# Moving one depthwise convolution's matmuls to the next slot, and the 5x5 convolution's transfers to one fixed point of each step

## The chip, the cores and the metric

The kernel runs on one core of a Trainium2 chip. The metric is the device time of one execution in microseconds (us); lower is better. PE is TensorE (matmuls, with PEld for its weight loads), DVE is VectorE, ACT is ScalarE, POOL is GpSimd and SP is SyncE. PE, DVE and ACT compute; SP and POOL issue nearly all the transfers here. [...]

## What is computed

The input is eight images of 32 channels by 128 x 128 pixels in float32. Two layers follow each other, each adding to its input. Cut to what matters:

```python
# layer 0
g    = group_norm(x)
xb   = patch_match_stack(g)        # per pixel, the 8 best of 25 shifts, gathered: 256 channels
dct  = conv1x1(xb, dct_w, groups=32)
h    = relu(depthwise3x3(conv1x1(xb, w1), w2))
h    = relu(depthwise3x3(conv1x1(h, w3), w4))
wien = sigmoid(depthwise3x3(conv1x1(h, w5), w6))
x    = x + conv1x1(conv1x1(wien * dct, inv_dct_w, groups=32), agg_w)
# layer 1
x    = x + conv5x5_each_channel(group_norm(x), kernel)
```

The three pairs (1x1, then depthwise 3x3) are called convolutions 1, 2 and 3 below. The product with `dct` and the aggregation that follows are the final part; layer 1 is the 5x5 convolution.

## The kernel before, in words

The work is a software pipeline over steps. A step `s` takes 8 rows of an image; an image has 17 steps (`NS + 1`), and there are 136 steps and two more to drain. In each step the loop `for i in (3, 2, 1, 0)` (L1026) runs four slots, named by `i`. Slot 3 runs the 1x1 of convolution 3 for the rows of two steps earlier, slot 2 that of convolution 2 for one step earlier, slot 1 that of convolution 1, and slot 0 the final part of two steps earlier. Every slot also gathers pixels for a later step.

The 256 channels of each convolution are halved. One half is depthwise-filtered on DVE: `pointwise_v` (L631, matmuls `pv`) puts it through ACT copies (L649) into a padded tile `tv`, `depthwise_v` (L681) runs nine taps, one on ACT (L692) and eight on DVE (L695), and L699 applies the activation. The other half is filtered on PE: `pointwise_t` (L651, matmuls `p`) goes through ACT copies (L672) into `t`, two SP transfers (L677, L679) copy rows of `t` to other partitions, and `depthwise_t` (L703) then runs 24 matmuls (L718, `pw<-t,dwd`), here called the taps of that convolution on PE. ACT evacuates them (L731), and SP copies two rows on (L620). After the DVE taps SP also copies two rows of `tv` (L627).

The taps on PE run one slot after their 1x1: generator `dt` is advanced twice per slot, once for the matmuls and once for L731 and L620. So convolution 3's taps stand in slot 2, convolution 2's in slot 1, convolution 1's in slot 0, and slot 3 has none. In PE's queue the slots are, without the tasks described next:

- slot 3: `pv` of convolution 3, `pa` (aggregation of the final part, L798), `p` of convolution 3, gather `pg` (L603)
- slot 2: `pv` and `p` of convolution 2, `pg`, taps of convolution 3
- slot 1: `pv` and `p` of convolution 1, `pg`, taps of convolution 2
- slot 0: `pc` (the grouped DCT, L777), `pg`, taps of convolution 1

All of `pv`, `p`, `pg`, `pc` and `pa` take turns in five PSUM buffers (`ps_x`, L71); the taps have two of their own (`ps_dw`, L193). DVE multiplies `pc` into the result (L785) in slot 0, and adds `pa` (L806) in slot 3.

Everything else, the search of the next image and the 5x5 of the image before, is cut into generator tasks. A task yields the letter of a queue and a cost, and is queued there: D for DVE, A for ACT, P and Q for PE. `run` (L222) takes tasks out. In each slot P runs after `pv`, then Q, then `tick` (L984) runs D tasks up to a credit (a share of 0.4 in slot 0, 0.2 in the others), then A. So a DVE task of slot 0 (a difference of images L413, costs L477 to L489, places L520 to L529, the 5x5's normalisation L864) is followed by its ACT part (such as the squares, L421) in slot 0, and by its PE part (`pd` L428, `pt` L494, `pi` L538, the 5x5's `p` L891) in slot 3.

The 5x5 (`layer1`, L815) takes eight channels at a time, four times per image: loads on POOL (`xy`, `xm`, L852 to L857), normalisation, matmuls, an add on DVE (L903) and four stores on POOL (L905), 62 rows each. The loads of the next eight channels reuse the two `xy` buffers that the stores read. For the last image (`last`) the loads are made at once.

PE, DVE and ACT keep the order in which the program was written (`ORDERED`, L14). POOL and SP do not: the tile scheduler orders their instructions by when it believes them ready.

Of the kernel before, what the change touches and what calls it, by code (L numbers as in the profile page):

```python
# [15 lines left out]
P = 128  # L16
# [26 lines left out]
def bm3d_conv_preact(  # L43
# [16 lines left out]
    nc = tc.nc  # L60
# [86 lines left out]
    with tc.tile_pool(name="setup", bufs=1) as sp, tc.tile_pool(  # L147
# [23 lines left out]
        for name, w in (("w1", w1), ("w3", w3), ("w5", w5)):  # L171
            t = sp.tile([P, 2, CK], F32, name=f"nat_{name}", tag=f"nat_{name}")
            nc.sync.dma_start(t, w.rearrange("(m p) i a b -> p m (i a b)", p=P))
            if name == "w1":

                nat, t = t, sp.tile([P, 2, CK], F32, name="w1_kc")
# [29 lines left out]

    queues = {"D": deque(), "A": deque(), "P": deque(), "Q": deque()}

    PAIR = 1.95
    pairs = [0]
# [9 lines left out]
    def run(which, credit=1e9):  # L222

        q, took = queues[which], 0.0
        for _ in range(len(q) if which != "D" else 1000):

            i = next(
                (
                    i
                    for i, (c, _, at) in enumerate(q)  # L230
                    if at <= now[0] and (c != PAIR or pairs[0] < 2)
                ),
                None,
            )
            if i is None or took >= credit:
                break
            cost, task, _ = q[i]
            del q[i]
            took += cost
            pairs[0] += cost == PAIR  # L240
            push(task)
        if which == "Q":
            pairs[0] = 0
        return took
# [570 lines left out]
    def layer1(b):  # L815

        yield "D", 0.2
        mv = work.tile([P, 2], F32, name=f"mv1_{b}", tag="mv1")
        nc.vector.bn_aggr(mv, stats[b].rearrange("p a b -> p (a b)"))
        mr = yield from group_stats(mv, f"b{b}")  # L820
        dg = work.tile([C, 2, C], F32, name=f"dg_{b}", tag="dg")
        for i in range(2):
            nc.vector.tensor_scalar(
                dg[:, i], ident[:C, :C], mr[:C, i : i + 1], None, op0=ALU.mult
            )
        yield "P", 0
        pb = ps_x.tile([P, 512], F32, name=f"pb_{b}", tag="x")
        nc.tensor.matmul(
            pb[:, : 2 * C], ones, dg.rearrange("p a b -> p (a b)"), start=True, stop=True
        )  # L830
        bc = work.tile([P, 2, C], F32, name=f"bc_{b}", tag="bc")
        nc.scalar.copy(bc.rearrange("p a b -> p (a b)"), pb[:, : 2 * C])
        last = b == NB - 1
        if last:
            ends = xnp.tile([P, HR, HX], F32, name="ends", tag="xn")
            ends = ends.rearrange("p r x -> p (r x)")[:, : 8 * 4 * W]
            ends = ends.rearrange("p (g c x) -> p g c x", g=8, x=W)
        xys = {}

        def load(c):  # L840


            if last:
                m = work.tile([P, 2, 4, W], F32, name=f"xo_{c}", tag="sel", bufs=4)
                t = [ends[:, c // 4], ends[:, c // 4 + 1], m[:, 0], m[:, 1]]
            else:
                t = [
                    work.tile([P, 4, W], F32, name=f"{name}_{b}_{c}_{e}", tag=name)
                    for name, e in (("xy", 0), ("xm", 0), ("xy", 1), ("xm", 1))
                ]  # L850
            src = x1d[b].rearrange("c y x -> y c x")
            nc.gpsimd.dma_start(t[0], src[:, c : c + 4])  # L852
            for h in range(2):
                nc.gpsimd.dma_start(
                    t[1][64 * h : 64 * h + 64], src[64 - 64 * h : P - 64 * h, c + 4 : c + 8]
                )
            nc.gpsimd.dma_start(t[2], src[:, c + 4 : c + 8])  # L857
            xys[c] = t

        def normalise(c):  # L860
            t = xys[c]
            for e in range(2):
                for i in range(4):
                    nc.vector.tensor_scalar(  # L864
                        t[3 - 2 * e][:, i],
                        t[e][:, i],
                        bc[:, 0, c + 4 * e + i : c + 4 * e + i + 1],
                        bc[:, 1, c + 4 * e + i : c + 4 * e + i + 1],
                        op0=ALU.subtract,
                        op1=ALU.mult,  # L870
                    )

        for c in range(0, C if last else 8, 8):
            load(c)
        push(middle(b, mr))
        for c in range(0, C, 8):
            if c == 0 or not last:
                yield "D", 2.0, 1 if last else 3
                normalise(c)
            yield "P", 0  # L880
            ps = [
                ps_x.tile([P, 4, W], F32, name=f"p5_{b}_{c}_{e}", tag="x") for e in range(2)
            ]
            t = xys.pop(c)

            for k, dx in enumerate((0, -2, -1, 1, 2)):
                xa, xz = max(0, -dx), min(W, W - dx)
                for h in range(2):
                    for e in range(2):
                        r, o = 64 * h, 64 * ((h + e) % 2)  # L890
                        nc.tensor.matmul(  # L891
                            ps[e][o : o + 64, :, xa:xz],
                            band[r : r + 64, dx + 2, r : r + 64],
                            t[3 - 2 * e][r : r + 64, :, xa + dx : xz + dx],
                            start=k == 0,
                            stop=k == 4,
                        )
            yield "D", 3.6 if last else 1.6
            if last and c + 8 < C:
                normalise(c + 8)  # L900
            for e in range(2):
                y = t[2 * e]
                nc.vector.tensor_add(y, y, ps[e])  # L903
                for a, z in ((0, 62), (66, P)):
                    nc.gpsimd.dma_start(  # L905
                        out[b, c + 4 * e : c + 4 * e + 4, a:z].rearrange("c y x -> y c x"),
                        y[a:z],
                    )
            if c + 8 < C and not last:
                yield "A", 0, 1  # L910
                load(c + 8)

        done.add((b, 0))

    def middle(b, mr):

        df = work.tile([P, SR, HX], F32, name=f"mid_{b}", tag="mid", bufs=1)
        for r in range(4):
            nc.gpsimd.dma_start(
                df[C * r : C * (r + 1), 0:5, 2 : 2 + W], x1d[b][:, 60 + r : 65 + r]  # L920
            )
        nc.gpsimd.memset(df[:, :, 0:2], 0.0)
        nc.gpsimd.memset(df[:, :, 2 + W :], 0.0)
        acc = df[:, 5, 2 : 2 + W]
        yield "D", 2.6, 4
        nc.vector.tensor_copy(acc, df[:, 2, 2 : 2 + W])
        nc.vector.tensor_scalar(
            df[:, 0:5, 2 : 2 + W],
            df[:, 0:5, 2 : 2 + W],
            mr[:, 0:1],  # L930
            mr[:, 1:2],
            op0=ALU.subtract,
            op1=ALU.mult,
        )
        for dy in range(5):
            if dy in (2, 4):
                yield "D", 2.0
            for dx in range(5):
                nc.vector.scalar_tensor_tensor(
                    acc,  # L940
                    df[:, dy, dx : dx + W],
                    kb[:, 5 * dy + dx : 5 * dy + dx + 1],
                    acc,
                    op0=ALU.mult,
                    op1=ALU.add,
                )
        for r in range(4):
            nc.gpsimd.dma_start(out[b, :, 62 + r], acc[C * r : C * (r + 1)])
        done.add((b, 1))
# [34 lines left out]
    def tick(b, i):  # L984

        now[0] += 1
        owed[0] += total / (NS - 2 if b else NS - 6) * (0.4 if i == 0 else 0.2)
        owed[0] -= run("D", owed[0]) if owed[0] > 0 else 0
        owed[0] = min(owed[0], 6.0)

    def until(cond, credit):
        while not cond():
            now[0] += 1
            run("D", credit)
            run("A")
            run("P")
            run("Q")

    with tc.manual_schedule(engines=ORDERED):
# [10 lines left out]

        dt = dv = kept = iter(())

        later = iter(())

        for s in range(len(steps) + 2):
# [10 lines left out]
            for i in (3, 2, 1, 0):  # L1026
                si = s - (i - 1 if i else 2)
                live = 0 <= si < len(steps)
                new_v = new_t = iter(())
                if live:  # L1030
                    bi, ni = steps[si]

# [13 lines left out]
                    final_dct(bi, ni, accs[3, bi, ni], xf, j0, j1)  # L1046

                run("Q")
                if s < len(steps):
                    unit(gather_select, u + 1, (0,))  # L1050
                    unit(gather_load, u + 3)
                    tick(b, i)
                next(later, None)
                next(new_v, None)
                if live and i:
# [1 line left out]
                next(kept, None)  # L1057
                if s < len(steps):
                    unit(gather_pixels, u)
                next(dt, None)  # L1060
                run("A")
                next(dv, None)
                if s < len(steps):
# [74 lines left out]
```

## Time and profile before

| | |
|---|---|
| median of 3 runs | 6853.36 us (6853.05 to 6886.87) |
| profiled execution | 6856.73 us, its span 6855.0 us |
| mean granted TensorE clock | 0.974 |
| PE busy | 6362.1 us, 93% |
| DVE busy | 5857.0 us, 85% |
| ACT busy | 5067.7 us, 74% |
| POOL busy | 3250.0 us, 47% |
| transfers | 1019.84 MB, mean 149 GB/s |
| taps on PE, L718 | 2161.7 us busy, 137.9 us idle just before |
| taps on DVE, L695 | 4032.8 us busy |

The page gives the busy time of an engine, groups of instructions by line with their mean duration, and the idle time of the engine just before them with what ended it. A view of the waits says who waited for whom, and a view in order of time shows single slots. One image in the steady part takes some 825 us: two successive first steps of an image stand at 1943 and 2768 us.

### The profile page before, as it was taken

What the parts mean: (1) busy time and instruction counts of PE and PEld (TensorE: products, weight loads), DVE (VectorE), ACT (ScalarE), POOL (GpSimd) and SP (SyncE); (2) the same over time, 40 slices, a digit from 0 to 9 for tenths busy, and PEclk for the clock granted to TensorE, in tenths of its full rate; (3) what the DMA queues carried; (4) which work ended last, traced back from release to release, by engine and by line L of the source; (5) the groups of instructions that cost most, each with busy time, mean ns of one, the idle gap of its engine ahead of it and who ended that gap; (6) DMA issues with size and microseconds to landing.
All of it is one profiled execution on the core that took longest, in us unless ns stands there. A gap on an engine that the chain in (4) does not pass through costs nothing.

```text
span 6855.0 us, 232443 instructions
## 1 busy us (share of the span) xinstructions
PE 6362.1 (93%) x101090; PEld 2969.2 (43%) x101090; DVE 5857.0 (85%) x8822; ACT 5067.7 (74%) x6698; POOL 3250.0 (47%) x5351
## 2 busy tenths in 40 slices
PE   4698899999999999999999999999999999999997
PEld 1344444444444444444444444444444444444443
DVE  6799988989889898988989888898988889877776
ACT  4687768777687777877778777887768777786772
POOL 6345436544464444644446444464445544344334
PEclk9899999999999999999999999999999999999998
DMA  3566656666566675665656656566665666566553
GB/s 80 134 151 148 155 134 150 163 149 162 149 155 161 147 168 134 167 145 151 165 131 165 160 145 167 134 172 152 151 153 146 161 157 149 137 164 157 148 151 79
DMA packets 809531, 1019.84 MB, mean 149 GB/s; under 512 B 255456, under 2 KB 619936, under 8 KB 808512
## 3 DMA queue, kind: packets, MB, share of 16 engines
q0 software_dynamic: 422432, 745.61, 42.4%
q1 hardware_dynamic: 381056, 256.86, 16.9%
q8 instruction: 796, 13.04, 0.8%
q10 hardware_dynamic: 5024, 2.49, 0.2%
q14 instruction: 223, 1.83, 0.1%
HBM read 553.25 MB, written 217.01 MB: 112 GB/s over the span
## 4 chain that ended last, share of the span: by engine, by line
PE 53%; DVE 20%; DMA 9%; ACT 8%; issue 6%; POOL 3%; SPq 0%; ACTq 0%; POOLq 0%; DVEq 0%
PE pw L718 19%; PE pv L641 13%; DVE acc L695 13%; PE p L665 11%; DMA t<-t 4%; PE pg L603 3%; PE pc L777 2%; PE p L891 2%; DVE idx L506 2%; ACT ib L588 2%; DVE df L413 1%; PE pd L428 1%; ACT df L421 1%; PE pa L798 1%; DVE acc L785 1%
## 5 line engine op out<-in xcount | busy, mean ns | idle before, releaser
L695 DVE SCALAR_TENSOR_TENSOR acc<-tv,dwv,acc 128x1024 f32<-128x1024 f32 (+3 forms) x3264 | 4032.8, 1237 | 255.1 <-ACT acc L692 141.7
L718 PE MATMUL pw<-t,dwd 96*32 96x508 f32 (+6 forms) x19392 | 2161.7, 593 | 137.9 <-DMA t<-t 97.4
L574 POOL DMA_DIRECT2D ib<-idxd x1024 | 571.8, 559 | 1828.0 <-ACT sel L589 1677.2
L718 PEld LDWEIGHTS pw<-t,dwd 96*32 96x32 f32 (+1 forms) x19392 | 715.7, 112 | 1265.5 <-issue 1174.2
L588 ACT ACTIVATE ib<-ib,nplace 128x1024 bf16<-128x1024 bf16 x1024 | 1170.3, 1143 | 19.1 <-DMA ib<-idxd 19.1
L589 ACT ACTIVATE sel<-ib 128x1024 f32<-128x1024 bf16 x1024 | 1084.7, 1059 | 32.5
L665 PE MATMUL p<-acc,lw 128*32 128x256 f32 x16768 | 991.3, 381 | 20.0 <-ACT tv L649 19.5
L641 PE MATMUL pv<-acc,lw 128*128 128x512 f32 (+1 forms) x2112 | 972.0, 602 | 30.2 <-DVE acc L785 22.9
L758 POOL DMA_DIRECT2D xf<-xbd x1088 | 652.8, 634 | 305.3 <-PE pc L777 80.7
L665 PEld LDWEIGHTS p<-acc,lw 128*32 128x32 f32 x16768 | 556.6, 111 | 447.8 <-ACT tv L649 59.5
L649 ACT COPY tv<-pv 128x512 f32<-128x512 f32 (+2 forms) x784 | 439.2, 578 | 403.4 <-PE pv L641 380.6
L603 PEld LDWEIGHTS pg<-sel,xt 128*32 128x32 f32 x45056 | 575.3, 111 | 260.4 <-ACT sel L589 67.1
L421 ACT ACTIVATE df<-df 128x786 f32<-128x786 f32 (+2 forms) x576 | 468.5, 860 | 291.6 <-DVE df L413 288.5
L603 PE MATMUL pg<-sel,xt 128*32 128x48 f32 x45056 | 593.5, 207 | 89.2 <-ACT sel L589 47.6
L731 ACT ACTIVATE acc<-pw 128x512 f32<-128x512 f32 (+2 forms) x808 | 442.7, 573 | 295.7 <-PE pw L718 294.9
L641 PEld LDWEIGHTS pv<-acc,lw 128*128 128x128 f32 x2112 | 380.0, 191 | 524.3 <-issue 404.4
L413 DVE TENSOR_TENSOR df<-xn 128x786 f32<-128x786 f32 (+2 forms) x576 | 527.8, 968 | 82.8 <-PE pd L428 70.9
L699 ACT ACTIVATE acc<-acc 128x1024 f32<-128x1024 f32 (+3 forms) x408 | 416.9, 1022 | 235.4 <-DVE acc L695 235.1
L672 ACT COPY t<-p 128x512 f32<-128x512 f32 x800 | 424.7, 571 | 127.8 <-PE p L665 125.8
L692 ACT ACTIVATE acc<-tv,dwv 128x1024 f32<-128x1024 f32 (+3 forms) x408 | 454.6, 1114 | 57.9 <-PE pa L798 39.1
L641 PE MATMUL pv<-xb,lw 128*128 128x512 f32 x1024 | 474.5, 606 | 0.0
L665 PE MATMUL p<-xb,lw 128*32 128x256 f32 x8192 | 467.6, 380 | 0.0
(151 smaller groups left out, 5778.6 us busy)
## 6 DMA issues: line engine op xcount, KB each, us to landing
ib<-idxd POOLq DMA_DIRECT2D x1024, 256.0 KB, 4.5
xbd<-xb POOLq DMA_DIRECT2D x128, 1024.0 KB, 6.8
xf<-xbd POOLq DMA_DIRECT2D x960, 128.0 KB, 7.0
t<-t SPq DMA_DIRECT2D x792, 128.0 KB
t<-t SPq DMA_DIRECT2D x384, 256.0 KB
tv<-tv SPq DMA_DIRECT2D x384, 130.0 KB
xt<-xtd POOLq DMA_DIRECT2D x240, 176.0 KB, 4.4
xl<-xs POOLq DMA_DIRECT2D x256, 64.0 KB, 2.5
```

Of the source, the lines that this page charges most:

```text
L413: nc.vector.tensor_sub(df[:, :, ca:cz], xn[:, r0 : r0 + SR, ca:cz], xn[:, r0 + dy : r0 + dy + SR, ca + dx : cz + dx],)
L421: nc.scalar.activation(df[:, :, ca:cz], df[:, :, ca:cz], AF.Square)
L574: nc.gpsimd.dma_start(ib.rearrange("p k y x -> p (k y x)"), idxd[b][s4 // 8, s4 % 8, 4 * k0 : 4 * k0 + 8] .rearrange("k x -> (k x)") .part ...
L588: nc.scalar.activation(ib, ib, AF.Square, bias=nplace)
L589: nc.scalar.activation(sel, ib, AF.Relu, scale=-1.0, bias=1.0)
L603: nc.tensor.matmul(pg[C * j : C * (j + 1), :, xa:xz], xt[:, t], sels[j // 2][:, j % 2, :, xa:xz], start=True, stop=True,)
L641: nc.tensor.matmul(ps[:, :hr], lhsT[:, g, P:CK], src(g)[:, h : h + hr], start=g == 0, stop=g == 1,)
L665: nc.tensor.matmul(ps[C * r : C * (r + 1), e, :nb], lhsT[:, g, s], rows[:, r : r + 4 * nb - 3 : 4], start=g == 0, stop=g == 1,)
L692: nc.scalar.activation(acc, rows, AF.Copy, scale=tap)
L695: nc.vector.scalar_tensor_tensor(acc, rows, tap, acc, op0=ALU.mult, op1=ALU.add)
L718: nc.tensor.matmul(pt[u][C * j : C * (j + 1), : nh[u], :nb, xa:xz], dwd[0:hi, i - 1, u, j, dx + 1], t[0:hi, j, : nh[u], :nb, xa + dx : xz ...
L758: nc.gpsimd.dma_start(xf[p : p + C, m, j0:j1], src[g, m, (h + m + 1) % 2, :, :, ya:yz])
```

## The change

Two things are moved; no arithmetic is added or removed.

- The taps of convolution 1 leave slot 0. Their generator is kept as `first_t` and advanced in slot 3 of the next step: the matmuls after the P and Q tasks and before `p` of convolution 3, the evacuation (L731) and the row copy (L620) after `tick`.
- A fifth queue, S, takes the 5x5's stores and loads (not those of the last image, but with the stores of its `middle` rows). It is run when slot 2 begins, and in `until`. Loads of the next eight channels come one S later than the stores. The two adds of L903 now stand together ahead of the stores.

```diff
-    queues = {"D": deque(), "A": deque(), "P": deque(), "Q": deque()}
+    queues = {"S": deque(), "D": deque(), "A": deque(), "P": deque(), "Q": deque()}
...
+        if not last:
+            yield "S", 0
         for c in range(0, C if last else 8, 8):
             load(c)
...
             for e in range(2):
+                nc.vector.tensor_add(t[2 * e], t[2 * e], ps[e])
+            if not last:
+                yield "S", 0
+            for e in range(2):
                 y = t[2 * e]
-                nc.vector.tensor_add(y, y, ps[e])
                 for a, z in ((0, 62), (66, P)):
                     nc.gpsimd.dma_start(
...
             if c + 8 < C and not last:
-                yield "A", 0, 1
+                yield "S", 0, 1
                 load(c + 8)
...
+        yield "S", 0
         for r in range(4):
             nc.gpsimd.dma_start(out[b, :, 62 + r], acc[C * r : C * (r + 1)])
...
             run("D", credit)
+            run("S")
             run("A")
...
+        first_t = iter(())
...
                 new_v = new_t = iter(())
+                if i == 2:
+                    run("S")
...
                 run("Q")
+                if i == 3:
+                    next(first_t, None)
                 if s < len(steps):
                     unit(gather_select, u + 1, (0,))
                     unit(gather_load, u + 3)
                     tick(b, i)
+                if i == 3:
+                    next(first_t, None)
...
-                next(dt, None)
+                if i:
+                    next(dt, None)
+                else:
+                    first_t, dt = dt, iter(())
                 run("A")
```

## The prediction

> **What bounds the kernel now.** I read the page's busy times first, then the waits of PE and DVE, then one step in order of time. Page:
>
> ```profile
> PE 6362.1 (93%) x101090; PEld 2969.2 (43%) x101090; DVE 5857.0 (85%) x8822; ACT 5067.7 (74%) x6698; POOL 3250.0 (47%) x5351
> ```
>
> PE is the bound: some 493 us of the 6855.0 are all it doesn't work in, and a stall of PE is paid in full unless it replaces another. Who PE and DVE waited for (total us, times, longest):
>
> ```profile
> PE pw L718 <- DMA t<-t: 97.4, 39, 5.1
> PE pd L428 <- ACT df L421: 42.9, 38, 2.9
> PE pv L641 <- DVE acc L785: 22.9, 15, 2.2
> PE p L665 <- ACT tv L649: 19.5, 7, 3.7
> ```
>
> and of DVE's waits the largest:
>
> ```profile
> DVE xr L806 <- PE pa L798: 311.8, 68, 15.7
> ```
>
> The taps' largest wait is for the row copies of `t`. I sorted PE's timeline by slots. Of 136 tap groups in slot 0, 16 came over 0.6 us late: 54.5 us idle before them, and 34.9 us by which they ran longer than the usual 5.33 us. In slot 2 it is 73.2 and 38.8 us (33 groups), in slot 1 almost nothing. One such step (start, duration, the wait in brackets), from slot 1's taps to slot 3's tasks:
>
> ```profile
> 3080.03 5.33 PE L718 MATMUL pw<-t,dwd 96*32 96x512 f32 x48
> 3085.30 1.95 PE L777 MATMUL pc<-xf,ldct 64*64 64x512 f32 x16
> 3087.17 1.12 PE L603 MATMUL pg<-sel,xt 128*32 128x48 f32 x88
> 3091.98 7.96 PE L718 MATMUL pw<-t,dwd 96*32 96x512 f32 x48 [3.69 <-DMA t<-t]
> 3099.87 3.70 PE L641 MATMUL pv<-acc,lw 128*128 128x512 f32 x8
> 3103.50 1.07 PE L798 MATMUL pa<-acc,lagg 128*32 128x256 f32 x16
> 3104.51 0.44 PE L538 MATMUL pi<-cst,oc 128*128 128x128 f32 x2
> ```
>
> SP's copies for slot 0's taps:
>
> ```profile
> 3079.78 0.59 SPq L677 DMA_DIRECT2D t<-t  x1
> 3080.41 1.68 SPq L679 DMA_DIRECT2D t<-t  x1
> ```
>
> POOL, with the stores of the 5x5:
>
> ```profile
> 3074.99 6.08 POOL L905 DMA_DIRECT2D out_dram<-xy  x4 [2.64 <-DVE xy L903]
> 3088.86 0.78 POOL L852 DMA_DIRECT2D xy<-x1d  x1 [7.79 <-DMA out_dram<-xy]
> ```
>
> DVE's product of the final part and the places of the search, and ACT's squares:
>
> ```profile
> 3087.13 2.48 DVE L785 TENSOR_TENSOR acc<-acc,pc 128x512 f32<-128x512 f32 x4
> 3095.49 0.42 DVE L529 TENSOR_TENSOR oc<-oc,cst 128x256 f32<-128x256 f32 x1
> ```
> ```profile
> 3092.17 1.74 ACT L421 ACTIVATE df<-df 128x786 f32<-128x786 f32 x2 [3.22 <-DVE df L413]
> ```
>
> The reader is to see two things. The stores go out at 3075, the row copies five us later take until 3092, and slot 0's taps wait. And the 5.33 us of taps between `pg` and `pv` are also what lets DVE and ACT finish slot 0's work before slot 3 needs it.
>
> **What the Trainium skill says.** "DMA: Bandwidth & Descriptors", section Issuing engines are not separate DMA queues: transfers of SP and POOL run on the same 16 DMA engines and interleave. The trace agrees: the SP copies above are late while POOL's stores are open. Same page, Why a DMA increments its semaphore by 16 and not by 1: a transfer is spread over the largest number up to 16 that divides its slowest dimension; 62 rows give 2 engines. The trace fits: a store of 124 KB lands in 10.9 us (median), a load of 256 KB on 128 rows in 4.1. "TensorE: Matmul & The Clock Gate", Part 1: the HAM clock gate: after an idle window TensorE runs slower until it has been busy again. The trace: after gaps of 2.5 us and more PE lost 1.6 to 2.7 us more in what followed, after shorter ones 0.4 to 0.6.
>
> **Part 1, removed: slot 0's waits.** Convolution 1's taps come behind `pv` (3.7) and `pa` (1.07), 4.8 us later; the longest wait there was 5.1. So 54.5 + 34.9 less 4.9 that waited for ACT: **-85**.
>
> **Part 2, removed: the old idle time of slot 3**, which is re-made below or covered by the taps now ahead of `p`: 23.1 (L785), 19.5 (L649), 13.8 (L421), 9.8 (`pi`), 14.4 (`pg`, no releaser shown): **-81**.
>
> **Part 3, added: `pv` of slot 3 comes straight behind slot 0's `pg`.** It takes the PSUM buffer that DVE's first L785 frees. From slot 1's start to that release: `pv` and ACT 5.5, eight DVE taps 10.5, L785 0.7 = 16.7. PE needs 13.4 for a bare slot 1 and 3.0 for slot 0 = 16.4. So 0.3 us a step where no task fills these slots, and less where one does. In the trace many L785 are up to 7.5 us later; since slot 3 grows by 5.3 us, I let DVE catch up that much. Over 125 steps this leaves 25 (no lateness but the excess over 5.33) to 80; I take **+45**.
>
> **Part 4, added: slot 3's tasks lose their cover.** They wait for DVE and ACT work of slot 0, and the taps come behind them. In the step shown, PE would be free at 3088.29 + 3.7 + 1.07 = 3093.0, while the places (L529) end at 3095.9: 2.9 us. The same sum for each of the 125 steps, DVE lateness taken off as in part 3, gives 104 us (14 an image: 2.4, 2.6, 3.1, 2.1, 1.7, ... and zeros). The instruction order of the changed kernel has other tasks in slot 0, among them an add, the middle rows and a cost block in one tick (8.4 us of DVE) ahead of a transposition. My count for one image is 13 to 17. **+104** (70 to 125). Some 60 such gaps slow what follows by 0.4: **+25** (10 to 40).
>
> **Part 5, SP's queue.** The order of the changed kernel has, in 108 of 128 steps, the `tv` copy of convolution 3 (L627) ahead of its `t` copies (L677, L679); in 12 before. The `tv` copy waits for five of the eight DVE taps, 6.6 us from their start. These start 10 to 11.4 us behind slot 3's start (rest of L785 1.9, tasks 8, which is 0.6 of a step's credit of 188 / 14, L806 and L807 0.85; or ACT's squares, activation, selection, L649 and L692). So L679 is issued by 19.4; the taps of slot 2 are due at 25.4 (slot 3 15.2, waits 1.3, slot 2's other matmuls 8.9). That leaves 6.0 us. In the trace the copies have 7 us; with over 5 us in hand 19 of 115 groups were late, with less 15 of 17, by 2.3 us. If a quarter of 108 steps fall under 5 us: 27 x 1.7 = **+45** (0 to 120; no gain, as nothing is issued earlier).
>
> **Part 6, the stores and loads.** S is run in slot 2, but POOL's order is the scheduler's. The order shows, per image, one group of stores straight behind slot 3's `x1d` writes (3 us ahead of convolution 3's copies), one behind 13 `dsum` loads, one split by `xr` loads, and one already in slots 1 and 0. The first kind has a likeness at 6182 us, where taps came 13 us after the first store, 1.5 late; I put 2 on it (0 to 6). The last delays the `xf` loads, as the stores in slot 0 do now, 2.5. The others 0.5 each. That is 5.5 an image against 2.4 such loss in slot 2 now, seven images: **+20** (-15 to +60). The PE cost of 5x5 tasks is unchanged; they are stretched over some ten steps instead of seven, which moves DVE work but adds none. L731 and L620 move along, hidden behind `p`; uncovered they cost 0.6 us of ACT each.
>
> **Sum.** -85 - 81 + 45 + 104 + 25 + 45 + 20 = +73. The profiled execution is 6856.7, 1.7 over its span and 3.4 over the median, so the sum is put on the median: 6853.4 + 73 = **6926**.
>
> **Rivals.**
> (a) *Faster.* DVE, freed of its 311.8 us wait for `pa` (which now comes 5.3 us earlier), runs ahead, and slot 0's tasks are ready when PE is. It decides at 4.75 us after `pg`: readiness under that and part 4 falls to 40 with 10 behind it, part 3 to 25, parts 5 and 6 to 0: -166 + 75 = -91, 6762. For it: 68 waits for `pa`. Against it: these tasks stand behind L785, which follows taps that PE itself releases.
> (b) *Cancelling.* SP's order does no harm (part 5 zero): +28, 6881. For it: 96 of 115 copies with over 5 us were in time.
> (c) *The stores now hit convolution 3 in full*: three groups an image at the 5.6 us that slot 0 paid, 21 x 5.6 = 118 in place of 20: 7024. For it: the first kind's position. Against it: the other two stand behind loads. Here the edit would not do what it says.
>
> **Chances.** Forecast 0.43, (a) 0.26, (b) 0.20, (c) 0.11. A measurement of this kernel can tell about 0.5% (34 us) from no change: faster 0.26, same 0.20, slower 0.54. The range takes in (a) nearly and (c) nearly: 6775 to 7010. Both signs hold chance; the forecast's own range is 6890 to 6990.
>
> **What would show it.** Right: slot 0 has no taps and no wait for `t<-t`; in slot 3 `pd`, `pi` and `pt` wait for L421, L529 and L489 by some 100 us in all; `pv` waits for L785 more than 22.9; slot 2's taps wait for `t<-t` longer than 43.9; the DVE wait for `pa` falls well under 311.8. Wrong: if slot 3's tasks wait under 50 us (part 4), or slot 2's taps wait no more than now (parts 5 and 6), the kernel is faster.

## The result, and the profile after

| | before | after |
|---|---|---|
| median of 4 runs | 6858.86 us (6853.05 to 6886.87) | 6986.86 us (6974.81 to 6997.43) |
| ratio, with 95% interval | | 1.0176 [1.0153, 1.0198] |
| span of the profiled execution | 6855.0 us | 6973.0 us |
| mean granted TensorE clock | 0.974 | 0.962 |

The kernel became slower by 128 us (medians; 118 by the spans). The forecast was 6926, slower by 73.

The page's first line after:

```profile
PE 6401.2 (92%) x101090; PEld 3042.0 (44%) x101090; DVE 5861.3 (84%) x8822; ACT 5079.7 (73%) x6698; POOL 3244.0 (47%) x5351
```

The matmuls are the same 101,090, yet PE is busy for 39 us more. The rest of the 118 us, some 79, is idle time of PE. What PE waited for after (total us, times, longest):

```profile
PE pw L718 <- DMA t<-t: 89.3, 37, 7.5
PE pv L641 <- DVE acc L785: 89.1, 66, 6.1
...
PE pt L494 <- issue: 42.5, 10, 5.8
PE pi L538 <- DVE oc L529: 41.6, 5, 20.3
PE pd L428 <- ACT df L421: 36.7, 43, 2.9
```

and of DVE's waits after:

```profile
DVE acc L695 <- ACT acc L692: 473.5, 203, 12.6
...
DVE xr L806 <- PE pa L798: 99.7, 38, 5.8
```

The row copies' wait is nearly what it was (97.4 before): slot 0's 49.1 us of it are gone, and slot 2's rose from 43.9 to 80.7. `pv` waits four times as long for L785 (22.9 before), and `pt` waits 42.5 us in ten places where it did not wait before. DVE waits 212 us less for `pa`, as forecast, but 332 us more for ACT's first tap L692 (141.7 before). That tap needs `pv`, and `pv` now waits for DVE: the two engines hold each other up in turn.

One step of after on PE, from the end of slot 0 to slot 2, shows it (start, duration, the wait in brackets):

```profile
4811.80 0.76 PE L603 MATMUL pg<-sel,xt 128*32 128x48 f32 x51
4815.21 3.67 PE L641 MATMUL pv<-acc,lw 128*128 128x512 f32 x8 [2.65 <-DVE acc L785]
4818.81 1.07 PE L798 MATMUL pa<-acc,lagg 128*32 128x256 f32 x16
4819.81 4.48 PE L893 MATMUL p<-xm,band 64*64 64x512 f32 x40
...
4825.79 5.30 PE L718 MATMUL pw<-t,dwd 96*32 96x512 f32 x48
...
4838.08 5.26 PE L641 MATMUL pv<-acc,lw 128*128 128x512 f32 x8 [2.60 <-DVE xy L904]
```

DVE in the same step:

```profile
4814.38 2.47 DVE L785 TENSOR_TENSOR acc<-acc,pc 128x512 f32<-128x512 f32 x4
...
4826.81 10.53 DVE L695 SCALAR_TENSOR_TENSOR acc<-tv,dwv,acc 128x1024 f32<-128x1024 f32 x8 [1.89 <-ACT acc L692]
4837.26 1.28 DVE L904 TENSOR_TENSOR xy<-xy,p 128x512 f32<-128x512 f32 x2
```

Two waits are to be seen. The first `pv` follows slot 0's `pg` with no taps between, so it waits until DVE's first L785 (4814.38 and 0.7) frees a buffer. The second `pv`, of slot 2, waits for the two buffers of the 5x5's `p`: their release, the add L904 (L903 before the change), stands behind all eight DVE taps. The forecast had the first wait and not the second.

A step in which a task of slot 3 waits, on PE and then on DVE:

```profile
4708.92 3.70 PE L641 MATMUL pv<-acc,lw 128*128 128x512 f32 x8
4712.56 1.07 PE L798 MATMUL pa<-acc,lagg 128*32 128x256 f32 x16
4719.39 1.08 PE L494 MATMUL pt<-cst,dsum 128*128 128x128 f32 x4 [5.76 <-issue]
4720.40 7.71 PE L718 MATMUL pw<-t,dwd 96*32 96x512 f32 x48
```
```profile
4710.39 3.84 DVE L944 SCALAR_TENSOR_TENSOR mid<-mid,kb 128x128 f32<-128x128 f32 x10
...
4718.06 1.23 DVE L489 TENSOR_TENSOR dsum<-dsum,v 128x1024 f32<-128x1024 f32 x1
```

The profile names no releaser for `pt` ("issue"), but it starts 0.1 us after L489, its input, ends. This is the tick that the forecast named, an add, the middle rows and a cost block ahead of a transposition. PE starts nothing of what stands behind `pt` in these 5.76 us. The taps that would have covered the wait now stand behind it, and they run for 7.71 us instead of 5.33. "TensorE: Matmul & The Clock Gate", Part 1 of the Trainium skill, says that after an idle window of about 3.4 us PE's clock is halved until PE has been busy for about as long; the trace agrees in kind, with 2.4 us lost after 5.76.

PE's idle time in us, sorted by slot (gaps over 0.06 us in PE's timeline from the first full step on, a slot beginning with its `pv`, or slot 0 with `pc`), with PE's busy time, from one profiled execution of each kernel. The experiments below are listed with it. Each ratio is to executions of the kernel before made beside it; their medians lay between 6859 and 6872 us.

| kernel | ratio to before | slot 3 | slot 2 | slot 0 | PE busy |
|---|---|---|---|---|---|
| before | 1 | 93.8 | 102.4 | 105.0 | 6362.1 |
| after | 1.0176 [1.0153, 1.0198] | 197.6 | 130.2 | 57.2 | 6401.2 |
| e1, S queue alone | 1.0079 [1.0062, 1.0096] | 77.4 | 188.0 | 100.3 | 6385.9 |
| e2, taps alone | 1.0093 [1.0075, 1.0111] | 204.4 | 96.0 | 54.6 | 6380.4 |
| e3, taps behind `pv` | 1.0173 [1.0158, 1.0187] | 280.1 | 100.2 | 49.2 | 6358.8 |
| e5, `tv` copy by ACT | 1.0138 [1.0121, 1.0155] | 200.5 | 113.4 | 60.5 | 6402.2 |
| e6, e1 with the add first | 1.0059 [1.0044, 1.0075] | 97.7 | 149.5 | 106.9 | 6360.8 |
| e8, stores alone held | 0.9988 [0.9978, 0.9999] | 88.6 | 98.0 | 113.1 | 6365.0 |
| e7, after with DVE credit moved | 1.0288 [1.0271, 1.0304] | 246.3 | 166.3 | 51.8 | 6427.5 |
| e11, after with early L785 | 1.0093 [1.0059, 1.0127] | 226.0 | 76.4 | - | 6379.9 |
| e4, before with split stores | 0.9848 [0.9833, 0.9862] | 82.4 | 104.1 | 65.9 | 6335.6 |
| e9, after with split stores | 1.0024 [1.0014, 1.0034] | 202.4 | 83.2 | 56.6 | 6374.2 |
| e10, e4 with `tv` copy by ACT | 0.9824 [0.9789, 0.9859] | 84.9 | 94.5 | 69.8 | 6325.4 |
| e12, e10 with early L785 | 1.0202 [1.017, 1.0234] | 31.9 | 47.8 | - | 6427.2 |

(In e11 and e12 `pc` stands in slot 1, so that slots 1 and 0 cannot be parted by it.) By this table the 118 us of the spans are made up so: slot 3 +104, slot 2 +28, slot 0 -48, PE's busy time +39; slot 1 and the ends make the small rest.

### The profile page after: what moved, and what is told of

It is laid out like the page before. It is cut to its first block, busy times and chain, and to the rows that moved or that the text cites. A ratio compares the mean times of both kernels' runs of the same rounds, so it can differ in the third digit from the quotient of the medians.

```text
span 6973.0 us, 232583 instructions
## 1 busy us (share of the span) xinstructions
PE 6401.2 (92%) x101090; PEld 3042.0 (44%) x101090; DVE 5861.3 (84%) x8822; ACT 5079.7 (73%) x6698; POOL 3244.0 (47%) x5351
## 4 chain that ended last, share of the span: by engine, by line
PE 30%; DVE 21%; DMA 7%; ACT 6%; issue 5%; POOL 3%; SPq 0%; DVEq 0%; POOLq 0%; ACTq 0%
DVE acc L695 16%; PE pw L718 11%; PE pv L641 8%; PE p L665 6%; DMA t<-t 3%; PE pg L603 2%; DVE acc L785 1%; ACT acc L692 1%; DVE df L413 1%; ACT df L421 1%; DMA xf<-xbd 1%; ACT tv L649 1%; DVE idx L506 1%; PE pa L798 1%; ACT ib L588 1%
## 5 line engine op out<-in xcount | busy, mean ns | idle before, releaser
L718 PE MATMUL pw<-t,dwd 96*32 96x508 f32 (+6 forms) x19392 | 2186.0, 595 | 110.1 <-DMA t<-t 89.3
L641 PE MATMUL pv<-acc,lw 128*128 128x512 f32 (+1 forms) x2112 | 1000.1, 617 | 116.0 <-DVE acc L785 89.1
L731 ACT ACTIVATE acc<-pw 128x512 f32<-128x512 f32 (+2 forms) x808 | 450.5, 574 | 522.9 <-PE pw L718 521.7
L665 PEld LDWEIGHTS p<-acc,lw 128*32 128x32 f32 x16768 | 586.6, 110 | 433.0 <-issue 83.7
L421 ACT ACTIVATE df<-df 128x786 f32<-128x786 f32 (+2 forms) x576 | 465.9, 860 | 236.9 <-DVE df L413 234.5
L413 DVE TENSOR_TENSOR df<-xn 128x786 f32<-128x786 f32 (+2 forms) x576 | 527.8, 967 | 78.8 <-PE pd L428 77.4
L692 ACT ACTIVATE acc<-tv,dwv 128x1024 f32<-128x1024 f32 (+3 forms) x408 | 454.4, 1114 | 34.5 <-PE pa L798 16.9
```

The source lines that it names most:

```text
L413: nc.vector.tensor_sub(df[:, :, ca:cz], xn[:, r0 : r0 + SR, ca:cz], xn[:, r0 + dy : r0 + dy + SR, ca + dx : cz + dx],)
L421: nc.scalar.activation(df[:, :, ca:cz], df[:, :, ca:cz], AF.Square)
L641: nc.tensor.matmul(ps[:, :hr], lhsT[:, g, P:CK], src(g)[:, h : h + hr], start=g == 0, stop=g == 1,)
L665: nc.tensor.matmul(ps[C * r : C * (r + 1), e, :nb], lhsT[:, g, s], rows[:, r : r + 4 * nb - 3 : 4], start=g == 0, stop=g == 1,)
L692: nc.scalar.activation(acc, rows, AF.Copy, scale=tap)
L718: nc.tensor.matmul(pt[u][C * j : C * (j + 1), : nh[u], :nb, xa:xz], dwd[0:hi, i - 1, u, j, dx + 1], t[0:hi, j, : nh[u], :nb, xa + dx : xz ...
```

## The experiments

**The two parts alone.** e1 undoes the move of the taps, e2 has nothing but it:

```diff
-                if i:
-                    next(dt, None)
-                else:
-                    first_t, dt = dt, iter(())
+                next(dt, None)
```

This is e1's edit to the changed kernel, the two calls of `next(first_t, None)` left out as well; e2 is the kernel before with just these lines of the change, without its queue S.

> Convolution 1's taps stay in slot 0, only the loads and stores of the 5x5 wait for slot 2. Theory (the moved taps cost the time: cover lost in slot 3, the tv copy ahead of the t copies): slot 0's wait for t<-t (49 us and some 35 us of longer running) goes for the most part, slot 3's waits stay near 94 us, slot 2's wait for t<-t stays near 44: 6790 to 6840 us. Rival (the new place of the stores costs the time): slot 2 waits for t<-t 80 us or more as in the changed kernel, little is won in slot 0: 6880 us or more.

> Only the taps are moved; loads and stores of the 5x5 are issued as before. Theory: pt, pi, pd wait in slot 3 some 90 us and pv for L785 some 89 us, slot 2 waits for t<-t over 60 us since the tv copy stands ahead of the t copies: 6930 to 7000 us, close to the changed kernel. Rival (stores): slot 2 waits under 50 us for t<-t, and the time is within 40 us of the kernel before, 6860 to 6900.

e1 took the time that the rival named, 6880 us or more (6928, a ratio of 1.0079), but not for its reason: slot 2's taps wait 48.9 us for `t<-t` and not 80. In e1, PE waits:

```profile
PE pw L718 <- DMA t<-t: 92.1, 32, 6.1
PE pv L641 <- DVE xy L904: 67.8, 12, 7.0
```

The row copies cost what they cost before; the new term is `pv` of slot 2 waiting for the 5x5's add, a wait that stood in neither expectation. The order of instructions says where it comes from: before, the 5x5's `p` stands in slot 3 in 13 of 29 cases and in slot 1 in 14; in e1 in slot 3 in 28 of 29. Loads that go out only when slot 2 begins fix the slot of everything that follows them: the 5x5 is locked to slot 3.

e2, at 1.0093 (6932 us), lies at the lower end of the theory's range: slot 3's idle time rose by 111 us. Its waits are others than the theory's: `pt`, `pi`, `pd` and `px` wait 57 us in slot 3 and not 90, `pt` not at all, and `pv` waits more than after:

```profile
PE pv L641 <- DVE acc L785: 126.8, 74, 6.1
```

So `pt`'s 42.5 us after come with the 5x5 that the queue S moves, and stand there in place of 38 us at `pv`. The two ratios multiply to 1.0173, so in sum no interaction of the parts is seen: about 0.8% for the held loads and stores and 0.9% for the taps.

**Is it the held loads?** e8 holds only the stores; e6 keeps e1's order but places the add where it can't hold `pv` up.

e8 is the kernel before with the stores in a task of their own, which yields S ahead of them (S is run as in the change):

```diff
             for e in range(2):
-                y = t[2 * e]
-                nc.vector.tensor_add(y, y, ps[e])
...
+                nc.vector.tensor_add(t[2 * e], t[2 * e], ps[e])
+            push(stores(c, t))
```

e6 is e1 with the add in a queue B, which is run right after `tick`:

```diff
-            yield "D", 3.6 if last else 1.6
+            yield ("D", 3.6) if last else ("B", 0)
```

> As the kernel before, but the stores of the 5x5 alone wait for slot 2; its loads go out as before, so its matmuls stay in the slots they had. Theory (holding the loads locks the 5x5 to slot 3, and that costs the time; the stores cost little): no wait of pv for the add, slot 0's wait for t<-t falls by 20 to 60 us, slot 2's rises by 0 to 20: 6800 to 6860 us, ratio 0.990 to 0.999. Rival (the stores in slot 2 cost as much as they did in slot 0, or more): ratio 1.000 to 1.008.

> As the run with only the loads and stores held for slot 2 (1.0079 of the kernel before), but DVE's add of the 5x5 is put straight behind the tasks of its own tick, ahead of the eight DVE taps, instead of in the queue of DVE tasks. Theory: that kernel loses its time at pv of slot 2, which waits 67.8 us in 12 steps for the add that frees its PSUM buffers; with the add ahead the wait goes, and PE's busy time falls with it: 6840 to 6865 us, ratio 0.996 to 1.000. Rival (the stores' place costs the time): ratio stays at 1.005 to 1.009.

e8 is 0.9988: with free loads the loss of e1 is gone, and the 5x5's `p` has its old slots (13 and 14). Its other half failed: slot 0's idle time did not fall (105.0 to 113.1). Of the 28 groups of stores, the 13 that had begun late in slot 0 now begin in slot 2 or just ahead of it. The 13 that begin in slot 1 stayed there, 14 to 18 us ahead of slot 0's late taps, as before: POOL's order is the scheduler's, and S did not hold these back.

e6 has the rival's ratio, 1.0059, though the wait for L904 is gone. The gain over e1, 0.2%, is not shown: the intervals overlap. Other waits took its place. In slot 3 `pd` waits 36.3 us for L439 (8.0 in e1) and `pi` 26.7 for L529 (8.4). And the taps wait longer than in e1 (92.1, and 16.8 with no releaser shown):

```profile
PE pw L718 <- DMA t<-t: 111.9, 41, 7.4
...
PE pw L718 <- issue: 46.7, 21, 7.8
```

The edit moved more than the add. An earlier add lets the stores go earlier: in e6, 19 of slot 2's 43 late tap groups follow a group of stores by less than 20 us and lost 58 us; in e1 it is 4 of 35, and 8 us. So in e6, unlike in e1, the place of the stores costs time, and e6 does not price the add's place alone. e1 and e8 show that holding the loads is what costs, and e1's largest new wait is the one for the add; what the locked 5x5 costs beyond it stays open.

**Which order of the taps in slot 3?** e3 has them straight behind `pv`, so that the tasks of slot 3 have their cover again.

```diff
+                if i == 3:
+                    next(first_t, None)
                 next(later, None)
                 if live and not i:
...
                 run("Q")
-                if i == 3:
-                    next(first_t, None)
```

> As the changed kernel, but the taps stand straight behind pv of slot 3, ahead of pa and of the P and Q tasks: the tasks have their cover of 5.33 us again, pv has not. Theory: waits of pt, pi, pd in slot 3 fall from some 95 to 25 us with 20 us of re-warming, the wait of pv for L785 stays at 80 to 100, and the order of SP is that of before, so slot 2's wait falls to 45: 6850 to 6900 us. Rival (the idle time of PE in slot 3 is DVE's lateness, which only shows at another matmul): the sum of slot 3's waits stays near 190 us and the time over 6950.

Nothing was won: 1.0173. The waits of `pt`, `pi` and `pd` did fall, and in their place e3 has (DVE's line first)

```profile
DVE xr L806 <- PE pa L798: 359.0, 70, 11.1
PE pv L641 <- DVE acc L785: 245.8, 95, 7.4
```

PE waits at `pv` for DVE, and DVE afterwards for `pa`, which stands behind `pv` and now behind the taps too. The rival is right that the wait changes its matmul and is not paid off, and wrong that its sum stays: slot 3's idle time rose from 198 to 280 us, while PE's busy time fell by 42. The same was tried from DVE's side:

e7 takes slot 1's credit for DVE tasks and gives it to slot 3:

```diff
-        owed[0] += total / (NS - 2 if b else NS - 6) * (0.4 if i == 0 else 0.2)
+        owed[0] += total / (NS - 2 if b else NS - 6) * (0.4 if i in (0, 3) else 0.2 if i == 2 else 0.0)
```

e11 makes the final product in slot 1, ahead of its `tick` and taps:

```diff
                 run("P")
-                if live and not i:
-                    final_dct(bi, ni, accs[3, bi, ni], xf, j0, j1)
+                if i == 1 and 0 <= s - 2 < len(steps):
...
+                    final_dct(*steps[s - 2], accs[(3, *steps[s - 2])], xf, j0, j1)
```

> As the changed kernel, but the credit for DVE's tasks of slot 1, which stand ahead of the taps that L785 follows, is given to slot 3 instead: L785 comes earlier by what those tasks take, 2.7 us in the mean. Theory (pv of slot 3 waits for the chain through L785, part 3 of the prediction): its wait falls from 89 to under 45 us; the tasks that now stand in slot 3 give back at most half of it: ratio to the kernel before 1.008 to 1.014 instead of 1.018. Rival (DVE is late for its sum of work, and the wait only changes its place): wait for L785 over 70 us, or gone with another of the same size; ratio 1.016 or more.

> As the changed kernel, but the product of the final part (pc on PE, L785 on DVE) is done in slot 1, ahead of slot 1's DVE tasks and taps, instead of in slot 0 behind them: pv of slot 3 has the buffers it needs long before it is due. Theory (L785's place in the chain behind the eight taps is what pv pays for): pv's wait for L785 falls from 89 to under 15 us, and pt, pi, pd of slot 3 keep their 90 us: ratio 1.003 to 1.008. Rival (DVE is late by the sum of its work at this point of the step, and the wait only moves to pt, pi, pd and p): ratio 1.012 or more, slot 3's idle time near 190 us.

e7 is the worst of all and on the rival's side: `pv` still waits 83.9 us for L785, in 83 instead of 66 places, and the tasks put into slot 3 add waits there and in slot 2. So it is not slot 1's tasks as such that make `pv` wait. e11 lies between the expectations. `pv` waits no more for L785, as the theory said, but slot 3's idle time did not fall (198 to 226): in e11 PE waits

```profile
PE pd L428 <- ACT df L421: 76.4, 54, 3.6
...
PE pt L494 <- DVE dsum L489: 53.2, 7, 7.7
...
PE pi L538 <- DVE mx L505: 37.1, 6, 6.2
PE pt L494 <- ACT tv L649: 36.4, 6, 6.3
```

where `pd` for L421 had 36.7 us after, `pt` 42.5 and, at the start of the kernel, 7.5, and `pi` for L505 18.9: the wait moved to the tasks. What e11 won, which no expectation had, is idle time of slot 2 (130 to 76 us), most of which slot 3 and the slots 1 and 0 gave back, and 21 us of PE's busy time.

**SP's queue.** e5 takes convolution 3's `tv` copy from SP, so that its `t` copies stand behind none.

```diff
-            nc.sync.dma_start(v[:, 0:2], v[:, R : R + 2])
+            queue = nc.scalar if i == 3 else nc.sync
+            queue.dma_start(v[:, 0:2], v[:, R : R + 2])
```

> As the changed kernel, but convolution 3's tv copy is issued by ACT two slots later instead of by SP, so that its t copies never stand behind it. Theory (part 5 of the prediction): slot 2's wait for t<-t falls from 81 to about 44 us and its longer running with it: 6935 to 6960 us. Rival (the stores in slot 2 delay the copies on the DMA engines): slot 2's wait stays at 70 us or more, time within 20 us of the changed kernel.

1.0138 against 1.0176: some 0.4%, 26 us by the ratios, as much as the theory's smallest; the two intervals just meet, and the profiled executions differ by 10 us. But slot 2's wait for `t<-t` stayed (80.7 to 79.5), as the rival said. What fell is its idle time by 17 us, as much as its taps waited in after for `tv<-tv` (9.8) and with no releaser shown (7.8). In the trace of after only six late groups had their `t` copies issued 4.4 us behind the matmul, as behind a `tv` copy, instead of 0.7; they are 2.3 to 3.7 us late, 18 us in all, and in e5 three of them remain, by 0.9 to 2.4. Ten others are due some 15 us behind stores of the 5x5 and are 2.7 to 7.5 us late, 44 us in all, and ten such groups stayed in e5.

**The stores.** e4 and e9 issue each store of 62 rows as one of 48 and one of 14, in before and in after:

```diff
-                for a, z in ((0, 62), (66, P)):
+                for a, z in ((0, 48), (48, 62), (66, 80), (80, P)):
```

> As the kernel before, but each store of the 5x5 on 62 rows is split into one of 48 and one of 14 rows. Theory (a store on 62 rows is carried by few DMA engines and holds up SP's row copies for its 10.9 us): it lands in under 6 us, slot 0's waits for t<-t and longer running fall from 84 to 30 to 50 us: 6800 to 6840 us, ratio 0.991 to 0.997. Rival (bytes and descriptors are the same, only POOL has four more to issue at 1.5 us each, or less each): ratio 0.998 to 1.004.

> As the changed kernel, but with the 62-row stores split into 48 and 14 rows. Theory (the stores in slot 2 hit convolution 3's copies in nine or ten groups of 3 to 6 us; the larger part of the changed kernel's loss is the lost cover and the 5x5 locked to slot 3, which this leaves): 40 to 60 us are won, ratio to the kernel before 1.008 to 1.012. Rival (the changed kernel loses its time mainly by the stores): ratio 1.000 or less.

e4 is faster than the kernel before by 1.5%, more than the theory's 0.3 to 0.9%. The DMA issues, before and then in e4 (KB each, median us from issue to landing):

```profile
out_dram<-xy POOLq DMA_DIRECT2D x112, 124.0 KB, 10.9
```
```profile
out_dram<-xy POOLq DMA_DIRECT2D x112, 96.0 KB, 2.4
...
out_dram<-xy POOLq DMA_DIRECT2D x112, 28.0 KB, 2.2
```

One store costs POOL 0.600 us to issue, two so 1.20, where the 62-row store took 1.513. Slot 0's wait for `t<-t` fell from 49.1 to 12.0 us, and none of its seven late tap groups follows a store closely, where 13 of 16 did (by 15 to 18 us). Of the 92 us between the spans slot 0's idle time is 39 and the shorter running of its taps 22. Another 16 are at the end of the kernel, where the last image's stores stand: from PE's last matmul to the end it is 27.9 us before and 12.0 in e4. The reason offered is the place that the prediction used ("DMA: Bandwidth & Descriptors", Why a DMA increments its semaphore by 16 and not by 1): a transfer is spread over the largest number of engines up to 16 that divides its slowest dimension, so 16 for 48 rows, 14 for 14, and 2 for 62. The section also names an exception for some copies that GpSimd issues; the 10.9 us speak against it for this store. The traces show the landing times and not the number of engines, and no run parts the shorter landing from POOL's shorter issue.

e9 missed both expectations: it wins as much over after (1.0176 to 1.0024, 1.5%) as e4 over before. The long stores cost the same in both kernels, wherever the queue S put them; 14 us of it are again the end of the kernel (26.3 to 12.7). And e9 is to e4 as after is to before (1.0024 / 0.9848 = 1.0179): with short stores, hence with little left in slot 0 for the move to save, the change costs the same 1.8%.

**Beyond e4.** e10 adds e5's edit to e4, e12 adds e11's as well.

> As the kernel before with the split stores (ratio 0.985), and convolution 3's tv copy issued by ACT instead of SP. Theory: the ten groups of slot 2 whose t copies were issued 4 to 6 us after the matmul because the tv copy stood ahead of them, some 20 us, are in time: ratio 0.981 to 0.984. Rival (ACT pays for the issue, 128 of them on an engine at 74%): 0.985 or more.

> As the kernel before with the split stores and convolution 3's tv copy on ACT, and the final product in slot 1. Theory: pv waits only 19 us for L785 where the taps stand ahead of it, so at most 20 us are won: ratio 0.979 to 0.983. Rival (L785 ahead of slot 1's taps makes these, and what stands behind them, 2.5 us later): ratio 0.986 or more.

e10 is the fastest by its median (6755.06 us), but its interval overlaps that of e4, so the gain of its second edit is not shown. e12 is slower by far: without `pc` in slot 0 the taps come 1.95 us earlier, and the wait for `t<-t` in slots 1 and 0 rises to 169.5 us in 69 places; `p` of slot 1, now behind `pc`, waits another 62.5 us for the products L786. The rival's bound was met, but neither expectation had these waits. Kept is e4 or e10.

## Why the prediction was right, and where not

The sign, the side of both stalls in slot 3 and the range were right; the size was 55 us short by the medians (61 against the forecast 6926, since the median of before is now 6858.86). By its steps:

- **Part 1, slot 0's waits, -85.** The wait went (idle time 105.0 to 57.2, -48). The 34.9 us of longer running did not: convolution 1's taps took 713.4 us in slot 0 and 743.6 in slot 3. They run long behind the waits of slot 3 too, as behind `pt` above, and slot 3 has more of them. So -85 was -18.
- **Parts 2, 3 and 4, idle time of slot 3: -81, +45 and +104, together +68.** Measured +104 (93.8 to 197.6). The tasks' waits (`pt` 42.5, `pi` 24.0, `pd` 23.2, `px` 5.8, in slot 3) sum to 95 and are the forecast's 104; `pv` for L785 is 89 where it had 45. The mis-sized step is "since slot 3 grows by 5.3 us, I let DVE catch up that much": DVE did not catch up. The 212 us that it no longer waits for `pa` it waits for L692, which follows `pv`. And parts 3 and 4 cannot be priced apart: e3 and e11 show that taking the wait from one matmul gives it to another.
- **Re-warming, +25.** PE's busy time rose by 39; of that the taps of slot 3 are 30, which the forecast had saved in part 1. The mechanism was right and stood in the sum with the wrong size.
- **Part 5, SP's queue, +45.** e5 gives some 26 by the ratios, 10 by the profiled executions: right in kind, smaller, since six groups were late by it (18 us) and not 27.
- **Part 6, stores and loads, +20.** This step failed: "The PE cost of 5x5 tasks is unchanged; they are stretched over some ten steps instead of seven, which moves DVE work but adds none." The queue S by itself costs 0.8%, 54 us, and not by its stores (e8): the held loads put all the 5x5 into slot 3, where its add stands behind the DVE taps with two of five PSUM buffers in hand. Against e2, which lacks S, after has 34 us more of idle time in slot 2, 19.6 of it at `pv` for the add, and 21 us more of PE's busy time; slot 3 has 7 us less. The stores themselves cost the same before and after (e4, e9), which the prediction did not consider: it asked where they would go and not why each takes 10.9 us.

A part of the size is luck. Sorted as in the table, the forecast is some +68 for slot 3, -50 for slot 0, -10 for PE's busy time (25 less the 34.9 of part 1) and +65 for slot 2 (parts 5 and 6, with some longer running in it). Measured are +104, -48, +39 and +28: too much in slot 2 made good for nearly half of what was missing in slot 3 and in the busy time.

Of the rivals, (a) was right in its first step (DVE's wait for `pa` fell from 311.8 to 99.7) and wrong in the second: DVE's freed time went into waiting for L692. (c), the stores hitting convolution 3, did happen in ten groups, 44 us in all, but it is not what made the kernel slower: with short stores the change costs the same 1.8% (e9 against e4). (b) is refuted by e5: with the `tv` copy out of the way the kernel still stands at 1.0138.

Open: how much of the locked 5x5's cost is its add (e6 left 0.6%, but moved the stores too), and how e11 won its time in slot 2.

## What to carry to other kernels

Work that fills an engine between two of its waits is cover for what stands behind it; before it is moved, ask what the other engine must finish in that time, and count the waits that take its place as one: of the three re-orderings tried here one won nothing (e3), one lost more (e7) and one won half of the loss back (e11), and in all three slot 3 waited longer than before them. Where a group of tasks is held for a fixed point of a loop, its later steps lose their spread too: look at which slot each of them falls into, and which buffers it then holds over which long instruction. And where transfers collide, first ask why they take so long: splitting 62 rows into 48 and 14 won 1.5% where moving them won nothing.

## What the hardware showed that was not expected

A store of 124 KB on 62 partitions took 10.9 us to land and POOL 1.513 us to issue; the same bytes as 48 and 14 rows landed in 2.4 and 2.2 us, and the two issues took 1.20 us together. PE ran the same taps 4% slower in slot 3 (743.6 against 713.4 us), behind the waits there, though all of them together were only some 200 us. Of 36 tap groups that began over 0.6 us late in after, 15 took some 7.0 us and 12 the usual 5.3.
